# Recording order of a two-layer convolution kernel: norms, loads and the pieces of the convolution

## The chip, the cores and the metric

The kernel runs on one core of a Trainium2 chip. The metric is the device time in microseconds (us) of one execution. The engines are TensorE (PE, with its weight loads PEld), VectorE (DVE), ScalarE (ACT), GpSimd (POOL) and SyncE (SP), which issues all the large transfers here.

## What is computed

Everything is float32. The input x has the shape (4, 256, 256, 64): batch, height, width, channels. The first layer is a Fourier branch and a depthwise convolution, each with a residual:

```python
h = _pw(_ln(x, g1, b1), w_te, b_te)                       # 64 -> 128 channels
F = jnp.fft.fft2(h.astype(jnp.complex64), axes=(1, 2))
fr = jnp.concatenate([jnp.real(F), jnp.imag(F)], axis=-1)
fc = jax.nn.gelu(_pw(fr, w_fc, b_fc), approximate=False)  # 256 -> 256
re, im = (fc[..., :HID], fc[..., HID:])
sp = jnp.real(jnp.fft.ifft2(re + 1j * im, axes=(1, 2)))
x1 = x + _pw(sp, w_tp, b_tp)                              # 128 -> 64
h2 = _pw(_ln(x1, g2, b2), w_fe, b_fe)                     # 64 -> 128
d = lax.conv_general_dilated(h2, w_dw, ...) + b_dw        # 3x3 depthwise
d = jax.nn.gelu(d, approximate=False)
return x1 + _pw(d, w_fp, b_fp)                            # 128 -> 64
```

The second layer treats the height as time. It takes a moving average over 25 steps as the trend, filters the rest in the frequency domain with one complex 128x128 matrix a channel, and adds the trend. For each channel this is one real 256x256 matrix, which the kernel builds from w_real and w_imag and then applies.

## The kernel before

The work falls into five streams, written as Python generators, which record instructions piece by piece and yield between pieces.

`forward_h(b)` (L312) goes over a batch in 32 chunks of 8 columns of the width. `load(q)` (L320) issues two transfers for xt and records the layer norm's statistics: the square on ACT (L295), two reductions and two small operations on DVE (L296 to L299). `transform(q)` (L331) records the scale on GpSimd, a power for rstd (L305) and a product that scales xt in place (L306), then four additions on DVE (xb L338 and xt L340), the matmuls ps_y (L345), two copies to yt on ACT (L352) and the stores to y_d (L357). xt has three buffers, xb one. One piece holds `load(q)` and then `transform(q - 1)`.

`spectral(b)` (L367) goes over 65 pairs of rows of the spectrum, in groups of two pairs. A group is loaded from y_d (L380), and GpSimd writes a negated copy (L399). A pair passes through `transform_w` (ps_x, L414, and a copy to xs), `mix` (ps_p, L434; the copy L447, sums L449, gelu L450, and half of L452 on DVE and half on GpSimd) and `project` (ps_z, L482), each one pair behind the other. `back_w` (ps_u, L499) closes a group with sums on DVE (L510, L511) and stores to u_d (L513). An iteration has three pieces; `transform_w` and `back_w` share the first.

`convolution(b)` (L548) goes over 32 chunks of 8 columns. `back_h(q)` loads uc and x1 (L561, L562), runs the matmuls ps_s (L569), adds them to x1 on DVE (L577, L581) and records the statistics. `to_channels(q)` scales into xn on GpSimd, sets the edges of tt to zero with a GpSimd memset (L591), transposes on TensorE (ps_t, L596), copies to tt on ACT (L603) and forms four row sums td on DVE (L610 to L615). `conv_first` and `conv_rest` make the convolution from four `product`s (ps_h, L629 and L639) whose results DVE folds into h (L660, L661, L667); `activate` is the gelu (L681), `finish` projects with ps_f (L690), adds x1 into st on DVE (L702) and stores to x2_d every second chunk. An iteration has five pieces, and a chunk is in flight for five iterations.

`matrices` (L742) makes the second layer's matrix for each of 64 channels: `first(c)` is ps_v and a copy to vs on ACT, `second(c)` is ps_m, an addition to mt on DVE (L780) and a store. `second` follows one channel behind `first`. The last part, behind the `seq` pool (L828), applies the matrices and isn't part of the change.

All tiles in PSUM come from one pool of eight banks (L118).

What sets the order is `spaced` and `merge` (L795, L800): each stream's pieces get equally spaced due times, in units of one batch, and the piece with the smallest due time is recorded next. Convolution b runs from b to b + 1, beside spectral b + 1 and forward transform b + 2. The recorded order is the order of priority; each engine then has its own queue[...].

Of the kernel before, what the change touches and what calls it, by code (L numbers as in the profile page):

```python
# [10 lines left out]
F32 = mybir.dt.float32  # L11
# [6 lines left out]
P = 128  # L18
N = 256
C = 64  # L20
# [86 lines left out]
def conv_seq_kernel(ctx: ExitStack, tc: tile.TileContext, a: dict, tables: bass.AP, out: bass.AP):  # L107
    nc = tc.nc
# [203 lines left out]
    def forward_h(b, pool):  # L312

        WH = 4
        y_d = spill.tile([P, N, 2, C], F32, tag="y_d", name=f"y_d_{b}")
        y_ds[b] = y_d
        flat = lambda t: t.rearrange("p t f w c -> p (t f w) c")
        chunks = {}

        def load(q):  # L320

            xt = pool.tile([P, 2, 2, WH, C], F32, tag="xt", name=f"xt_{b}_{q}", bufs=3)
            for hf in range(2):
                w0 = hf * P + q * WH
                nc.sync.dma_start(
                    xt[:, :, hf],
                    x[b, :, w0 : w0 + WH, :].rearrange("(t p) w c -> p t w c", p=P),
                )
            chunks[q] = xt, statistics(pool, flat(xt), f"{b}_{q}")

        def transform(q):  # L331
            n = f"{b}_{q}"
            xt, var = chunks.pop(q)
            xb = pool.tile([P, 2, 2, WH, C], F32, tag="xb", name=f"xb_{n}", bufs=1)
            yt = pool.tile([P, 2, WH, 2, C], F32, tag="yt", name=f"yt_{n}")
            scale(pool, flat(xt), flat(xt), var, n)
            for i, op in enumerate((ALU.add, ALU.subtract)):
                nc.vector.tensor_tensor(xb[:, :, i], xt[:, :, 0], xt[:, :, 1], op)  # L338
            for i, op in enumerate((ALU.add, ALU.subtract)):
                nc.vector.tensor_tensor(xt[:, i], xb[:, 0], xb[:, 1], op)  # L340
            for m in range(2):
                ps = bank(f"ps_y_{n}_{m}")

                for i in range(2):
                    nc.tensor.matmul(  # L345
                        ps[i * C : (i + 1) * C],
                        dh[:, m, i * C : (i + 1) * C],
                        xt[:, i].rearrange("p f w c -> p (f w c)"),
                        start=True,
                        stop=True,  # L350
                    )
                nc.scalar.copy(  # L352
                    yt[:, :, :, m, :], ps.rearrange("p (f w c) -> p f w c", f=2, c=C)
                )
            for par in range(2):
                w0 = par * P + q * WH
                nc.sync.dma_start(y_d[:, w0 : w0 + WH], yt[:, par])  # L357

        NCH = P // WH
        for q in range(NCH + 1):  # L360
            if q < NCH:
                load(q)
            if q >= 1:
                transform(q - 1)
            yield

    def spectral(b, pool):  # L367
# [163 lines left out]
        for i in range(len(prs) + 3):  # L531
            if i < len(prs):
# [4 lines left out]
                transform_w(pr)  # L537
            if 0 <= i - 3 < len(prs) and prs[i - 3]["last"]:
                back_w(prs[i - 3]["g"])
# [8 lines left out]
    def convolution(b, pool):  # L548
# [5 lines left out]
        x1s, ts, stores = {}, {}, {}  # L554
        rows = lambda t: t.rearrange("p t w c -> p (t w) c")

        def back_h(q):
# [6 lines left out]
            )  # L564

            pss = [bank(f"ps_s_{n}_{i}") for i in range(2)]
# [15 lines left out]
            x1s[q] = x1, statistics(pool, rows(x1), n)  # L582

        def to_channels(q):

            n = f"c_{b}_{q}"
            x1, var = x1s[q]
            xn = pool.tile([P, 2, W, C], F32, tag="xn", name=f"xn_{n}", bufs=1)
            scale(pool, rows(x1), rows(xn), var, n)
            tt = pool.tile([P, NP, N + 2], F32, tag="tt", name=f"tt_{b}_{q}", bufs=1)  # L590
            nc.gpsimd.memset(tt[:, :, 0 : N + 2 : N + 1], 0.0)  # L591
            for j in range(0, NP, 2):
# [12 lines left out]
                )  # L605

# [76 lines left out]
        def finish(q, i0):  # L683
# [16 lines left out]
            x1 = x1s[q][0]  # L700
# [13 lines left out]

        for q in range(NCH + 4):
            if q < NCH:
                back_h(q)
            yield
            if 0 <= q - 1 < NCH:
                to_channels(q - 1)  # L720
            yield
            done = 0 <= q - 4 < NCH
            now = 0 <= q - 3 < NCH
# [3 lines left out]
            if done:  # L727
                finish(q - 4, 0)
            if now:
                conv_rest(q - 3, 0)  # L730
            yield
# [3 lines left out]
            if done:  # L735
                finish(q - 4, 2)
                del gs[q - 4], x1s[q - 4]
            yield
# [3 lines left out]
    def matrices(pool):  # L742
# [17 lines left out]
        def first(c):  # L760
# [3 lines left out]
            vs = pool.tile([P, 2, N], F32, tag="vs", name=f"vs_{c}", bufs=3)  # L764
# [18 lines left out]
        pending = None  # L783
        for c in range(C):
            if c % CG == 0:
                load(c)
            done = first(c)
            if pending is not None:
                second(*pending)
            pending = done  # L790
            yield
        second(*pending)
        yield
# [21 lines left out]
    with tc.tile_pool(name="fwd", bufs=2) as fwd, tc.tile_pool(name="mix", bufs=2) as mixing:  # L815
        at = {
            all_batches(spectral, mixing, 3 * 68, -1.0, -0.08): -1.0,
            all_batches(forward_h, fwd, 33, -2.05, -1.1): -2.05,
        }
        with tc.tile_pool(name="matrices", bufs=2) as pool:  # L820
            at[spaced(matrices(pool), C + 1, -2.05, -1.1)] = -2.05
            merge(at, -1.0)
        with tc.tile_pool(name="conv", bufs=2) as conv:
            at[all_batches(convolution, conv, 5 * 36, 0.0, 1.0)] = 0.0
# [86 lines left out]
```

## Time and profile before

| | |
|---|---|
| median of 3 runs | 5897.06 us (5895.28 to 5897.61) |
| the profiled execution | 5904.44 us, span 5902.7 us |
| granted TensorE clock, mean | 0.945 of full speed |
| busy: PE, PEld, DVE, ACT, POOL | 92%, 59%, 65%, 39%, 30% of the span |
| moved by DMA | 653.73 MB, 111 GB/s over the span |

Busy times are of the engines' instructions. A matmul's end is modelled and its neighbours overlap, so a PE that is busy is not one at its peak; the granted clock is a column of its own in the views cut by time. Waits are shown as an engine's idle time ahead of an instruction, with the instruction on another engine that ended it.

### The profile page before, as it was taken

Reading aid. Unit: us, or ns where it says so; the run is one execution under the profiler, and the core shown is the slowest. Engines: PE = TensorE matmul, PEld = TensorE weight load, DVE = VectorE, ACT = ScalarE, POOL = GpSimd, SP = SyncE. Lnnn points to the kernel's source line nnn. Section 1 sums busy time; section 2 is a strip of 40 time slices with the busy share of each in tenths; the row PEclk is TensorE's granted clock in tenths of the full one; section 3 lists DMA queues with packets and bytes.
Section 4 is the critical chain, followed back from the end, with each engine's and each line's share of the span. In section 5 each row is a group of like instructions: output and inputs, shape, how many; then the busy total and the mean of one; then the engine's idle time right before and its main releaser. Section 6 shows DMA issues by size and latency. Waiting matters only on the chain.

```text
span 5902.7 us, 72524 instructions
## 1 busy us (share of the span) xinstructions
PE 5436.0 (92%) x27467; PEld 3470.5 (59%) x27467; DVE 3814.1 (65%) x6039; ACT 2276.8 (39%) x3162; POOL 1744.8 (30%) x1038
## 2 busy tenths in 40 slices
PE   7878988798999989899999989999999989997999
PEld 3446656556665656566656556676667656664444
DVE  5555656576777767676777766677766667774221
ACT  2224545444443434344444434444444422221211
POOL 3443333343333233333333322222222223330000
PEclk9988989899999989999999889999999999998999
DMA  4552323322322322322322222222222122224998
GB/s 151 164 166 86 101 86 100 97 83 90 104 97 86 99 73 91 113 79 93 100 97 88 91 79 83 72 82 76 90 76 86 59 78 86 86 86 132 334 321 270
DMA packets 654916, 653.73 MB, mean 111 GB/s; under 512 B 31117, under 2 KB 506719, under 8 KB 654440
## 3 DMA queue, kind: packets, MB, share of 16 engines
q1 hardware_dynamic: 654568, 649.09, 34.7%
q8 instruction: 219, 3.59, 0.3%
q14 instruction: 129, 1.06, 0.1%
HBM read 363.76 MB, written 285.21 MB: 110 GB/s over the span
## 4 chain that ended last, share of the span: by engine, by line
PE 54%; issue 16%; POOL 12%; DVE 10%; DMA 3%; ACT 3%; SPq 1%; POOLq 0%; DVEq 0%; ACTq 0%
PE ps_h L629 12%; PE ps_o L851 7%; PE ps_h L639 7%; PE ps_f L690 6%; PE ps_z L482 5%; PE ps_x L414 4%; POOL rstd L305 4%; PE ps_u L499 4%; POOL xt L306 3%; PE ps_p L434 3%; PE ps_s_c L569 3%; DVE g L449 2%; POOL rstd_c L305 2%; DVE xb L338 2%; PE ps_y L345 1%
## 5 line engine op out<-in xcount | busy, mean ns | idle before, releaser
L629 PE MATMUL ps_h<-td,wc_main 128*128 128x512 f32 x2048 | 1063.1, 642 | 77.6 <-DVE h L661 72.4
L450 ACT ACTIVATE g<-g,b_fc 128x1024 f32<-128x1024 f32 (+1 forms) x520 | 591.9, 1142 | 767.9 <-DVE g L449 767.6
L305 POOL TENSOR_TENSOR rstd_c<-var_c,minus_half 128x16 f32<-128x16 f32 x128 | 419.6, 3278 | 1316.2 <-DVE var_c L299 1224.6
L452 POOL TENSOR_TENSOR g<-g 128x512 f32<-128x512 f32 x260 | 334.0, 1284 | 1448.2 <-ACT g L450 1389.5
L449 DVE TENSOR_TENSOR g<-ps_p,g 128x512 f32<-128x512 f32 x1040 | 687.5, 681 | 75.6 <-ACT g L447 65.4
L639 PEld LDWEIGHTS ps_h<-td,wc_half 64*128 64x128 f32 x4032 | 426.8, 193 | 487.6 <-issue 421.1
L482 PEld LDWEIGHTS ps_z<-w_tp,g 128*128 128x128 f32 x4064 | 509.0, 203 | 225.5 <-POOL g L452 70.3
L482 PE MATMUL ps_z<-w_tp,g 128*128 128x64 f32 x4064 | 548.1, 290 | 99.8 <-POOL g L452 64.8
L629 PEld LDWEIGHTS ps_h<-td,wc_main 128*128 128x128 f32 x2048 | 367.7, 199 | 420.7 <-issue 314.8
L639 PE MATMUL ps_h<-td,wc_half 64*128 64x128 f32 (+1 forms) x4032 | 604.7, 416 | 0.0
L338 DVE TENSOR_TENSOR xb<-xt 128x512 f32<-128x512 f32 x256 | 214.8, 866 | 566.4 <-POOL xt L306 549.0
L667 DVE TENSOR_TENSOR h<-h,ps_h 128x512 f32<-128x512 f32 x512 | 338.6, 683 | 346.7 <-PE ps_h L639 346.6
L690 PE MATMUL ps_f<-w_fp,h 128*128 128x64 f32 x4096 | 525.2, 283 | 38.4 <-DVE h L661 35.8
L434 PE MATMUL ps_p<-xs,wp 64*128 64x512 f32 (+1 forms) x2080 | 531.0, 610 | 28.4 <-DVE h L661 22.7
L681 ACT ACTIVATE h<-h,b_conv 128x1024 f32<-128x1024 f32 x256 | 281.5, 1142 | 690.9 <-DVE h L679 690.4
L690 PEld LDWEIGHTS ps_f<-w_fp,h 128*128 128x128 f32 x4096 | 493.5, 197 | 91.1 <-issue 47.3
L414 PE MATMUL ps_x<-tab,yb 128*128 128x128 f32 x4064 | 537.9, 288 | 0.8 <-DVE ut L511 0.8
L414 PEld LDWEIGHTS ps_x<-tab,yb 128*128 128x128 f32 x4064 | 498.6, 200 | 53.6 <-issue 25.9
L851 PE MATMUL ps_o<-xc,mt 128*128 128x512 f32 x1024 | 450.1, 602 | 42.7 <-issue 21.8
L499 PE MATMUL ps_u<-zt,tab 128*128 128x256 f32 x2048 | 474.5, 386 | 12.0 <-ACT zt L485 11.9
L305 POOL TENSOR_TENSOR rstd<-var,minus_half 128x16 f32<-128x16 f32 x128 | 379.3, 2963 | 322.3 <-DVE var L299 320.2
L447 ACT COPY g<-ps_p 128x512 f32<-128x512 f32 (+1 forms) x520 | 297.8, 582 | 451.2 <-PE ps_p L434 448.9
(120 smaller groups left out, 6863.8 us busy)
## 6 DMA issues: line engine op xcount, KB each, us to landing
xt<-in_x_dram SPq DMA_DIRECT2D x256, 256.0 KB, 3.7
y_d<-yt SPq DMA_DIRECT2D x256, 256.0 KB, 3.3
yb<-y_d SPq DMA_DIRECT2D x256, 256.0 KB, 3.3
x_c<-in_x_dram SPq DMA_DIRECT2D x128, 512.0 KB, 4.8
u_d<-ut SPq DMA_DIRECT2D x256, 256.0 KB, 2.3
uc_c<-u_d SPq DMA_DIRECT2D x128, 512.0 KB, 4.5
x_d<-st SPq DMA_DIRECT2D x128, 512.0 KB, 3.9
xc<-x_d SPq DMA_DIRECT2D x64, 1024.0 KB, 10.3
```

The costliest lines, as they stand in the source:

```text
L305: nc.gpsimd.tensor_tensor(rstd, var, minus_half.to_broadcast([P, n]), ALU.pow)
L414: nc.tensor.matmul(ps[:, j * N + t * P : j * N + (t + 1) * P], blk[:, t, k, lo : lo + 2 * C], tb[:, t, :], start=i == 0, stop=i == 1,)
L434: nc.tensor.matmul(ps[:, :nf], wp[rows, cols], rhs[rows], start=True, stop=r == 1 or not pr["special"],)
L449: nc.vector.tensor_tensor(g[:, i], pss[0][:, :nf], g[:, 1], op)
L450: nc.scalar.activation(g, g, AF.Gelu, bias=b_fc[:, half : half + 1])
L482: nc.tensor.matmul(zv[:, j, 2 * t + r, :], lhs(d, j, t), w_tp, start=True, stop=True)
L499: nc.tensor.matmul(ps[:, r * KG * C : (r + 1) * KG * C], tb[:, t, :], zt[:, t, ri].rearrange("p k c -> p (k c)"), start=ri == 0, stop=ri == 1,
L629: nc.tensor.matmul(pss[par], wc_main[:, par, k, :], ts[q][:, k].rearrange("p j i -> p (j i)"), start=True, stop=False,)
L639: nc.tensor.matmul(pss[par][:, s * P : (s + n) * P], wc_half[lo : lo + C, k, :], td[lo : lo + C, k, at : at + n, :].rearrange("p j i -> p ...
L667: nc.vector.tensor_tensor(g, g, m, (ALU.add, ALU.subtract)[r])
L690: nc.tensor.matmul(pv[:, t, 2 * i + par, :], gs[q][par][:, i0 + i, t * P : (t + 1) * P], w_fp, start=True, stop=True,)
L851: nc.tensor.matmul(ps[:, :nf], mt[:, c % CM, t, to * P : (to + 1) * P], xc[:, t, b0 : b0 + nb2, :, c % CG, :], start=t == 0, stop=t == 1,)
```

## The change

The forward transform's norm, statistics and scale together, becomes a step of its own, `norm(q)`. One chunk takes two pieces: first `transform(q - 1)`, then `load(q + 1)` and `norm(q)`. The first load comes ahead of the loop.

The spectral part yields between `transform_w` and `back_w`, so an iteration has four pieces.

In the convolution `load` is separated from `back_h` and recorded a chunk ahead; the norm is separated from `back_h` and `to_channels` and stands two pieces after `back_h`; the row sums are separated from the transposes. An iteration has nine pieces. The tile tt is allocated once a batch, and its edges are zeroed once by DVE instead of once a chunk by GpSimd.

In `matrices`, `second` follows two channels behind `first`, and vs has four buffers. The counts of pieces given to `spaced` follow.

```diff
@@ forward_h
-            chunks[q] = xt, statistics(pool, flat(xt), f"{b}_{q}")
+            chunks[q] = xt
+
+        def norm(q):
+            n = f"{b}_{q}"
+            xt = flat(chunks[q])
+            scale(pool, xt, xt, statistics(pool, xt, n), n)
 
         def transform(q):
             n = f"{b}_{q}"
-            xt, var = chunks.pop(q)
+            xt = chunks.pop(q)
...
-            scale(pool, flat(xt), flat(xt), var, n)
...
+        load(0)
         for q in range(NCH + 1):
-            if q < NCH:
-                load(q)
             if q >= 1:
                 transform(q - 1)
+            yield
+            if q + 1 < NCH:
+                load(q + 1)
+            if q < NCH:
+                norm(q)
             yield
@@ spectral
                 transform_w(pr)
+            yield
             if 0 <= i - 3 < len(prs) and prs[i - 3]["last"]:
                 back_w(prs[i - 3]["g"])
@@ convolution
-        def back_h(q):
+        def load(q):
...
+            x1s[q] = x1
+            ucs[q] = uc
+
+        def back_h(q):
+
+            n = f"c_{b}_{q}"
+            uc, x1 = ucs.pop(q), x1s[q]
...
-            x1s[q] = x1, statistics(pool, rows(x1), n)
+
+        def norm(q):
+            n = f"c_{b}_{q}"
+            xns[q] = pool.tile([P, 2, W, C], F32, tag="xn", name=f"xn_{n}", bufs=1)
+            scale(pool, rows(x1s[q]), rows(xns[q]), statistics(pool, rows(x1s[q]), n), n)
+
+        tt = pool.tile([P, NP, N + 2], F32, tag="tt", name=f"tt_{b}", bufs=1)
+        nc.vector.memset(tt[:, :, 0 : N + 2 : N + 1], 0.0)
 
         def to_channels(q):
 
-            n = f"c_{b}_{q}"
-            x1, var = x1s[q]
-            xn = pool.tile([P, 2, W, C], F32, tag="xn", name=f"xn_{n}", bufs=1)
-            scale(pool, rows(x1), rows(xn), var, n)
-            tt = pool.tile([P, NP, N + 2], F32, tag="tt", name=f"tt_{b}_{q}", bufs=1)
-            nc.gpsimd.memset(tt[:, :, 0 : N + 2 : N + 1], 0.0)
+            xn = xns.pop(q)
...
+
+        def row_sums(q):
...
+        load(0)
         for q in range(NCH + 4):
-            if q < NCH:
-                back_h(q)
-            yield
-            if 0 <= q - 1 < NCH:
-                to_channels(q - 1)
-            yield
-            done = 0 <= q - 4 < NCH
-            now = 0 <= q - 3 < NCH
+            new, old = q < NCH, 0 <= q - 4 < NCH
+            before, now = 0 <= q - 1 < NCH, 0 <= q - 3 < NCH
             if now:
                 conv_first(q - 3)
             yield
-            if done:
+            if old:
                 finish(q - 4, 0)
+            yield
+            if before:
+                to_channels(q - 1)
+            yield
             if now:
                 conv_rest(q - 3, 0)
+            yield
+            if before:
+                row_sums(q - 1)
+            yield
+            if new:
+                back_h(q)
             yield
             if now:
                 conv_rest(q - 3, 1)
                 activate(q - 3)
-            if done:
+            yield
+            if new:
+                norm(q)
+            yield
+            if old:
                 finish(q - 4, 2)
                 del gs[q - 4], x1s[q - 4]
+            if q + 1 < NCH:
+                load(q + 1)
             yield
@@ matrices
-            vs = pool.tile([P, 2, N], F32, tag="vs", name=f"vs_{c}", bufs=3)
+            vs = pool.tile([P, 2, N], F32, tag="vs", name=f"vs_{c}", bufs=4)
...
-        pending = None
-        for c in range(C):
-            if c % CG == 0:
-                load(c)
-            done = first(c)
-            if pending is not None:
-                second(*pending)
-            pending = done
-            yield
-        second(*pending)
-        yield
+        pending = []
+        for c in range(C + 2):
+            if c < C:
+                if c % CG == 0:
+                    load(c)
+                pending.append(first(c))
+            if c >= 2:
+                second(*pending.pop(0))
+            yield
@@ the counts of pieces
-            all_batches(spectral, mixing, 3 * 68, -1.0, -0.08): -1.0,
-            all_batches(forward_h, fwd, 33, -2.05, -1.1): -2.05,
+            all_batches(spectral, mixing, 4 * 68, -1.0, -0.08): -1.0,
+            all_batches(forward_h, fwd, 2 * 33, -2.05, -1.1): -2.05,
...
-            at[spaced(matrices(pool), C + 1, -2.05, -1.1)] = -2.05
+            at[spaced(matrices(pool), C + 2, -2.05, -1.1)] = -2.05
...
-            at[all_batches(convolution, conv, 5 * 36, 0.0, 1.0)] = 0.0
+            at[all_batches(convolution, conv, 9 * 36, 0.0, 1.0)] = 0.0
```

More of the change, by code (lines that the diff above doesn't have):

```diff
@@ L553, in convolution @@
         NP = W // 2
-        x1s, ts, stores = {}, {}, {}
+        x1s, ucs, xns, ts, stores = {}, {}, {}, {}, {}
         rows = lambda t: t.rearrange("p t w c -> p (t w) c")
-        def back_h(q):
+        def load(q):
             n = f"c_{b}_{q}"
@@ L699, in finish @@
                 stores[s] = pool.tile([P, 2, C, SW], F32, tag="st", name=f"st_{b}_{s}")
-            x1 = x1s[q][0]
+            x1 = x1s[q]
             for t in range(2):
```

## The prediction

> **What bounds the kernel now.** I read the page's busy table first (PE 92%, DVE 65%, no other engine above 40%), then the windows view cut at the stage borders of the trace, then the waits, then the timeline of one stage that repeats. The borders are the copies at L391, which open a batch of the spectral part (417, 1118, 2365, 3641 us), and the last edge columns at L677 (4780, 5405 us).
>
> ```profile
> core 0: us, PE busy (x) PEld busy (x) DVE busy (x) ACT busy (x) POOL busy (x), PEclk, DMA share, GB/s
> 0.00:417.00 417.00, 322.54 (x1051) 173.08 (x1051) 227.75 (x393) 102.51 (x167) 169.98 (x78) 0.93 0.50 158
> 417.00:1118.00 701.00, 603.62 (x3298) 433.35 (x3300) 428.80 (x637) 353.93 (x509) 252.43 (x159) 0.90 0.32 98
> 1118.00:2365.00 1247.00, 1140.39 (x6108) 745.90 (x6105) 887.34 (x1385) 525.52 (x726) 432.85 (x257) 0.93 0.29 90
> 2365.00:3641.00 1276.00, 1185.45 (x6396) 775.57 (x6394) 912.65 (x1436) 535.88 (x740) 425.40 (x254) 0.94 0.29 92
> 3641.00:4780.00 1139.00, 1131.66 (x6499) 781.05 (x6499) 784.15 (x1254) 494.75 (x668) 280.54 (x196) 0.99 0.25 79
> 4780.00:5405.00 625.00, 601.68 (x3097) 364.34 (x3096) 476.20 (x810) 176.31 (x226) 183.56 (x95) 0.98 0.22 76
> ```
>
> Call these stages A to F (the last stage, up to 5903, is G). To see how far each is from a full TensorE I take the pace of its matmul groups from the timeline, start of a group to start of the next with nothing waiting: ps_y 1.87 us a forward chunk; ps_x 1.89, ps_p 1.82, ps_z 1.85 and half of ps_u's 3.55, so 7.4 a spectral pair; ps_s 1.82, ps_t 0.92, four products of 2.98 and ps_f 3.7, so 18.4 a convolution chunk; 3.45 a channel of the matrices. Per batch that is 60 (32 chunks), 480 (65 pairs) and 586 (32 chunks); the matrices are 221. Work against time taken: A 281 and 28 of preparation against 417, excess 108; B 540 against 701, 161; C 1126 against 1247, 121; D 1126 against 1276, 150; E 1066 against 1139, 73; F 586 against 625, 39. TensorE is the bound, and some 650 us are lost to it before G. Part of that is its clock: the clock is 0.99 in E, where it hardly stops, and 0.90 in B.
>
> The difference between D and E is one stream: E has no forward transform. Where it runs, DVE is blocked by one wait (in us, times, longest), which has no entry in E or F; TensorE's own waits of the whole run stand under it.
>
> ```profile
> DVE xb L338 <- POOL xt L306: 549.0, 123, 7.7
> ```
>
> ```profile
> PE ps_h L629 <- DVE h L661: 72.4, 18, 5.3
> PE ps_z L482 <- POOL g L452: 64.8, 34, 5.2
> PE ps_m L772 <- ACT vs L765: 47.8, 23, 3.9
> PE ps_f L690 <- DVE h L661: 35.8, 9, 5.7
> PE ps_y L345 <- issue: 25.9, 3, 10.2
> PE ps_p L434 <- DVE h L661: 22.7, 15, 4.4
> ```
>
> The reader is to see that TensorE's own waits name DVE's h (L661), which frees its PSUM banks, while DVE's queue stands 4.5 us at a time (549/123) behind an xb that wants GpSimd's scaled xt. How that comes about shows in A, DVE first and GpSimd after it:
>
> ```profile
> 189.77 1.29 DVE L338 TENSOR_TENSOR xb<-xt 128x512 f32<-128x512 f32 x2 [4.99 <-POOL xt L306]
> 191.10 1.29 DVE L340 TENSOR_TENSOR xt<-xb 128x512 f32<-128x512 f32 x2
> 192.31 0.68 DVE L780 TENSOR_TENSOR mt<-t,ps_m 128x512 f32<-128x512 f32 x1
> 192.91 1.21 DVE L296 TENSOR_REDUCE total<-xt 128x16 f32<-128x1024 f32 x1
> 194.04 1.21 DVE L298 TENSOR_REDUCE squares<-sq 128x16 f32<-128x1024 f32 x1
> ```
>
> ```profile
> 196.21 2.89 POOL L305 TENSOR_TENSOR rstd<-var,minus_half 128x16 f32<-128x16 f32 x1 [6.47 <-DVE var L299]
> 199.18 1.90 POOL L306 TENSOR_TENSOR xt<-xt,rstd 128x1024 f32<-128x1024 f32 x1
> ```
>
> The two engines take turns: 6.4 us of DVE, then 5.0 us (2.89 + 1.90 and handing over) of GpSimd, 11.35 us a chunk, while TensorE has 8.8 us of work in it (two channels and a ps_y).
>
> [...]xb is 866 ns on average against a median of 691, so the overlap that the change wants has a price of up to some 0.2 us an instruction.
>
> **The change part by part.**
>
> Forward transform. The scale (rstd and xt) leaves the piece that uses it and is recorded half a chunk earlier, with the statistics; the load stands a chunk before them, at SP behind the y_d stores of the chunk before, which wait for yt. No instruction is added. What can go is the 549 us of DVE's wait. The order of each engine in the trace is not simply the recorded one (at 2517.66 us squares L298 runs ahead of total L296, recorded the other way), so the record is a priority and part of the wait will stay. Per stage, with the xb waits 167, 137, 126 and 124 us in A to D:
> - C and D: I let them come to E's excess over work, 1139/1066 = 1.068, so 1203 each: 44 and 73 us saved. E is the same program without the stream that blocks.
> - B: the DVE load is heavier for its length, and ps_z waits for g L452 besides (62 us), which shares GpSimd with the scale. I take half of its excess: 80.
> - A: DVE's and GpSimd's turns can overlap only if the next chunk's reductions stand between a scale and its xb. Three xt buffers allow it. Bounds: 0 (turns stay) and 87 (417 to the 330 that 1.068 gives). I take 25.
>
> Matrices. second(c) comes two channels after first(c), one more vs buffer. It removes up to the 47.8 us of ps_m's wait, all in A. While A is paced by the turns, this saves nothing; it is inside A's 25.
>
> Convolution, pieces. Nine instead of five, no instruction more. Products no longer follow each other without spectral work between, so DVE has longer to free banks; the waits for h L661 (131 us over C and D) are in the 117 already counted. E has none of them, so I count E at 0, with bounds of -15 and +25. norm stands two pieces after back_h and four before to_channels: at some 39 us an iteration about 17 us, against 3 us of reductions and 5.5 us of GpSimd (3.28 + 2.18). If that cover failed, ps_t would wait some of those 5.5 us in each of 128 chunks; now it waits 35 us in all. xn has one buffer, free when the transposes of the chunk before have run, half an iteration earlier.
>
> Convolution, loads. Two DMAs of 512 KB (4.5 us to land) go behind the x2_d stores, which wait for DVE's st, and have most of an iteration. TensorE waits for uc only 7.3 us now: 0 saved.
>
> Edge zeros. 128 GpSimd memsets (13.8 us, with 31.3 us of waiting for td in front) become four on DVE; edge_rows L679 at 0.2 us is the nearest row, so under 1 us. ps_t and ps_z wait 19.5 us for the memset, most of it in F. I take 15.
>
> The yield between transform_w and back_w spreads ps_x and ps_u: 0, inside the above.
>
> Sum: 25 + 80 + 44 + 73 + 15 = 237 us. The profiled execution took 5904.4 us (span 5902.7), so 5667; it lies 7 above the median of the runs, so 5660.
>
> **Rivals.**
>
> All of it: A, B, C and D all come to 1.068 (87 + 124 + 44 + 73) and the memset's 15: 343 us, 5554. For it: DVE is 55 to 72% busy in A to D, so nothing but order stands in the way. Against it: in B and A the loop scale, xb, ps_y, store, next load runs through every engine[...].
>
> The order hardly changes: since the record is only a priority, the scale already runs as soon as var is there (rstd follows var within 0.25 us in A), and xb is still placed right behind it. Then only the memset and some bank waits go, 15 + 25: 5857.
>
> Slower: the scale, now early, stands in GpSimd's queue in front of the subtraction g L452 for which ps_z waits. There are 256 norms, each 4.8 to 5.5 us. Today those waits are 65 us in 34 places. If half of the main case's gain (118 us) is still there, it decides from 0.46 us of added waiting a norm (118/256); at 0.85 us, a sixth of a norm, it adds 218 us and the kernel ends 100 us above the 5897. For it: g L452 has 1.27 us of work and sits directly between gelu and ps_z. Against it: ps_z is recorded five spectral pieces after mix, over 20 us in C and D. I put this case at 6000, and at 1.3 us a norm it would be 6110.
>
> **How the numbers follow.** Main case 0.43, all of it 0.12, hardly any 0.22, slower 0.23. Its own range for the main case is 5560 to 5790 (A at its two bounds, B between 40 and 124, E -15 to +25). No change means within 0.2% of 5897, which is what a measurement here can tell. Hardly-any falls faster in 0.13, within in 0.06, slower in 0.03. So faster 0.68, same 0.06, slower 0.26. The range 5520 to 5950 leaves out most of the slower case and the edge of the full one, about 0.2.
>
> **What would show it.** Right: the wait of xb for xt falls from 549 us to below 250, the waits for h L661 from 131 to below 50, PE's clock in C and D rises to about 0.97, the tt memset is gone from GpSimd, D takes about as long as E plus a forward transform. A's period of 11.35 us tells whether the turns ended. Wrong: xb still waits 4 to 5 us a chunk (hardly any), or ps_z waits for g L452 well above 65 us (slower).

## The result and the profile after

The changed kernel takes 5931.2 us (median of 4 runs, 5929.4 to 5932.3) beside 5897.3 us for the kernel before in the same series (4 runs, 5895.3 to 5899.0): ratio 1.0057, 95% interval 1.0040 to 1.0075. It is slower by 34 us (0.6%), where 5660 us, a gain of 237 us, was forecast. The profiled executions have spans of 5930.5 and 5902.7 us, so they show 28 us of it.

The windows view of the changed kernel, cut at the same events as before (the DVE copy of yr, now L399; the last edge columns, now L696):

```profile
core 0: us, PE busy (x) PEld busy (x) DVE busy (x) ACT busy (x) POOL busy (x), PEclk, DMA share, GB/s
0.00:417.00 417.00, 323.24 (x1051) 168.60 (x1051) 227.20 (x394) 102.00 (x166) 166.69 (x75) 0.93 0.49 155
417.00:1122.00 705.00, 604.73 (x3285) 439.86 (x3286) 429.48 (x636) 354.91 (x508) 256.23 (x162) 0.89 0.32 99
1122.00:2377.00 1255.00, 1142.36 (x6122) 764.38 (x6122) 857.59 (x1373) 520.85 (x723) 396.58 (x220) 0.92 0.29 90
2377.00:3677.00 1300.00, 1194.39 (x6408) 797.17 (x6408) 892.41 (x1445) 537.14 (x742) 411.58 (x226) 0.93 0.29 90
3677.00:4808.00 1131.00, 1118.37 (x6493) 775.29 (x6493) 782.08 (x1259) 490.87 (x670) 263.23 (x165) 0.99 0.25 79
4808.00:5426.00 618.00, 592.35 (x3058) 358.15 (x3057) 464.44 (x803) 174.32 (x225) 153.58 (x64) 0.97 0.24 77
```

A is unchanged at 417 us, B 4 us longer, C 9 and D 24 longer, E 8 to 9 shorter. (The border between F and G in the prediction, 5405 us, lay 6 us behind the last edge columns, which start at 5398.8; with the right border F took 618 us before and takes 618 now.) The loss therefore sits in C and D, where the forward transform runs beside the convolution; with B these were the stages that were to gain most. TensorE's clock there did not rise to 0.97; it fell from 0.93 and 0.94 to 0.92 and 0.93.

Next the waits of the changed kernel, first the one entry that was to shrink, then the head of TensorE's own list (us in total, times, longest):

```profile
DVE xb L342 <- POOL xt L306: 740.2, 128, 9.5
```

```profile
PE ps_z L490 <- POOL g L460: 66.9, 34, 4.7
PE ps_t L613 <- POOL xn_c L306: 65.7, 10, 10.4
PE ps_t L613 <- DVE h L680: 53.2, 16, 7.3
PE ps_y L349 <- issue: 40.0, 5, 12.4
PE ps_m L802 <- DVE mt L810: 34.3, 22, 2.2
PE ps_p L442 <- DVE ut L519: 31.7, 14, 3.3
PE ps_h L648 <- DVE ut L519: 24.9, 4, 7.5
```

The reader is to see two things. The wait of DVE for the scaled xt grew from 549 to 740 us, in all 128 chunks. And the products of the convolution no longer wait for their own banks: ps_h, ps_f and ps_p for h (131 us before) are gone from this list, as forecast. But other matmuls wait for other DVE work instead (ps_t for h, ps_p and ps_h for ut): together the three come to 110 us, and ps_z for h, a little further down the list, adds 19.5. So 131 us of waiting have become 129 under other names: DVE, which frees these banks, still stands at xb.

How the wait grew is in the timeline of D. GpSimd first (start, length, engine, line, what; idle time before it in brackets), then DVE, then the one matmul group of that stretch that waited:

```profile
2536.09 2.90 POOL L305 TENSOR_TENSOR rstd_c<-var_c,minus_half 128x16 f32<-128x16 f32 x1 [18.47 <-DVE var_c L299]
2539.06 2.35 POOL L306 TENSOR_TENSOR xn_c<-x_c,rstd_c 128x1024 f32<-128x1024 f32 x1
2541.38 2.89 POOL L305 TENSOR_TENSOR rstd<-var,minus_half 128x16 f32<-128x16 f32 x1
2544.35 1.91 POOL L306 TENSOR_TENSOR xt<-xt,rstd 128x1024 f32<-128x1024 f32 x1
```

```profile
2538.25 0.16 DVE L299 SCALAR_TENSOR_TENSOR var<-var,squares 128x16 f32<-128x16 f32 x1
2538.36 0.69 DVE L457 TENSOR_TENSOR g<-ps_p,g 128x512 f32<-128x512 f32 x1
2538.97 0.68 DVE L460 TENSOR_TENSOR g<-g 128x512 f32<-128x512 f32 x1
2546.29 2.75 DVE L342 TENSOR_TENSOR xb<-xt 128x512 f32<-128x512 f32 x2 [6.63 <-POOL xt L306]
```

```profile
2551.83 3.65 PE L490 MATMUL ps_z<-w_tp,g 128*128 128x64 f32 x16 [6.22 <-DVE h L680]
```

DVE makes var at 2538.25, does two more instructions and comes to xb. GpSimd has only begun the convolution's norm: the forward norm stands behind it and starts 3 us after var, so the two norms run back to back for 10 us and DVE stands for 6.63 us. Behind xb in DVE's queue wait the h additions that free PSUM banks: their matmuls on ps_h have ended by 2542.9, and they start at 2550.28, after the 6.63 us and the four additions of transform. TensorE then stands 6.22 us for one of them.

Stage A has the same turns as before:

```profile
191.68 1.29 DVE L342 TENSOR_TENSOR xb<-xt 128x512 f32<-128x512 f32 x2 [4.99 <-POOL xt L306]
...
203.04 1.29 DVE L342 TENSOR_TENSOR xb<-xt 128x512 f32<-128x512 f32 x2 [4.99 <-POOL xt L306]
```

The period is 203.04 - 191.68 = 11.36 us, against 11.35 before: the sign that the prediction named for the turns not having ended.

Where xb really stands in DVE's queue can be counted in the traces, as the DVE instructions that ran between the last var of a chunk and its xb (means over the 32 chunks of a batch, batches 0 to 3):

```
before                 0.4   1.1   2.1   2.6
after                  0.3   1.3   1.1   1.4
forward part alone     0.2   1.1   2.0   2.5
convolution alone      0.4   1.1   1.5   2.1
```

The scale and the statistics are now recorded a piece of work ahead of xb, yet xb runs as close behind var as before. In the kernel before, the statistics of the next chunk were even recorded ahead of xb, and xb did not run behind them either; the new loop records `transform(q - 1)` first and the next `norm(q)` after it, so it no longer asks for that order. And in batches 2 and 3 the forward rstd stands directly behind an instruction of the convolution's norm on GpSimd in 22 and 23 of 32 chunks, where before it was 8 and 8.

### The profile page after: what moved, and what is told of

The parts are those of the page before. It is cut to its first block, busy times and chain, and to the rows that moved or that the text cites. A ratio compares the mean times of both kernels' runs of the same rounds, so it can differ in the third digit from the quotient of the medians.

```text
span 5930.5 us, 72294 instructions
## 1 busy us (share of the span) xinstructions
PE 5433.2 (92%) x27467; PEld 3507.2 (59%) x27467; DVE 3752.8 (63%) x6043; ACT 2270.3 (38%) x3162; POOL 1647.9 (28%) x910
## 5 line engine op out<-in xcount | busy, mean ns | idle before, releaser
L648 PE MATMUL ps_h<-td,wc_main 128*128 128x512 f32 x2048 | 1014.1, 618 | 33.0 <-DVE ut L519 24.9
L458 ACT ACTIVATE g<-g,b_fc 128x1024 f32<-128x1024 f32 (+1 forms) x520 | 591.5, 1143 | 669.0 <-DVE g L457 668.5
L342 DVE TENSOR_TENSOR xb<-xt 128x512 f32<-128x512 f32 x256 | 199.4, 812 | 740.2 <-POOL xt L306 740.2
L490 PE MATMUL ps_z<-w_tp,g 128*128 128x64 f32 x4064 | 565.5, 296 | 107.8 <-POOL g L460 66.9
L490 PEld LDWEIGHTS ps_z<-w_tp,g 128*128 128x128 f32 x4064 | 528.1, 209 | 221.6 <-POOL g L460 72.1
L305 POOL TENSOR_TENSOR rstd_c<-var_c,minus_half 128x16 f32<-128x16 f32 x128 | 370.8, 2897 | 885.1 <-DVE var_c L299 799.2
L658 PE MATMUL ps_h<-td,wc_half 64*128 64x128 f32 (+1 forms) x4032 | 588.3, 407 | 0.0
L422 PE MATMUL ps_x<-tab,yb 128*128 128x128 f32 x4064 | 557.0, 294 | 9.3 <-DVE g L457 8.7
L422 PEld LDWEIGHTS ps_x<-tab,yb 128*128 128x128 f32 x4064 | 518.8, 207 | 48.0 <-DVE g L457 10.6
L709 PEld LDWEIGHTS ps_f<-w_fp,h 128*128 128x128 f32 x4096 | 506.9, 201 | 66.4 <-issue 19.5
L507 PEld LDWEIGHTS ps_u<-zt,tab 128*128 128x128 f32 x2048 | 384.5, 193 | 74.7 <-ACT zt L493 11.7
```

Of the source, the lines that this page charges most:

```text
L305: nc.gpsimd.tensor_tensor(rstd, var, minus_half.to_broadcast([P, n]), ALU.pow)
L422: nc.tensor.matmul(ps[:, j * N + t * P : j * N + (t + 1) * P], blk[:, t, k, lo : lo + 2 * C], tb[:, t, :], start=i == 0, stop=i == 1,)
L458: nc.scalar.activation(g, g, AF.Gelu, bias=b_fc[:, half : half + 1])
L490: nc.tensor.matmul(zv[:, j, 2 * t + r, :], lhs(d, j, t), w_tp, start=True, stop=True)
L507: nc.tensor.matmul(ps[:, r * KG * C : (r + 1) * KG * C], tb[:, t, :], zt[:, t, ri].rearrange("p k c -> p (k c)"), start=ri == 0, stop=ri == 1,
L648: nc.tensor.matmul(pss[par], wc_main[:, par, k, :], ts[q][:, k].rearrange("p j i -> p (j i)"), start=True, stop=False,)
```

## The experiments

18 kernels were run. Ratios are to the kernel before, run beside each. In the table A to D are stage lengths and the last column is the whole wait of xb, all in us.

| kernel | time | ratio, 95% interval | A | B | C | D | xb waits |
|---|---|---|---|---|---|---|---|
| before | 5897 | 1 | 417 | 701 | 1246 | 1276 | 549 |
| after | 5931 | 1.0057 [1.0040, 1.0075] | 417 | 705 | 1255 | 1300 | 740 |
| fwd_only | 5921 | 1.0039 [1.0026, 1.0052] | 421 | 698 | 1252 | 1285 | 512 |
| conv_only | 5839 | 0.9901 [0.9888, 0.9915] | 418 | 702 | 1210 | 1260 | 676 |
| fwd_conv | 5853 | 0.9927 [0.9915, 0.9939] | 422 | 699 | 1219 | 1267 | 706 |
| yield_only | 5913 | 1.0032 [1.0020, 1.0043] | 418 | 711 | 1241 | 1279 | 585 |
| no_fwd | 5901 | 1.0009 [1.0000, 1.0017] | 417 | 709 | 1240 | 1283 | 702 |
| no_yield | 5858 | 0.9939 [0.9925, 0.9953] | 418 | 707 | 1215 | 1264 | 699 |
| no_mat | 5933 | 1.0065 [1.0049, 1.0080] | 422 | 711 | 1255 | 1297 | 744 |
| order_before | 5771 | 0.9787 [0.9774, 0.9800] | 338 | 630 | 1255 | 1287 | 14 |
| order_fwd | 5573 | 0.9452 [0.9437, 0.9467] | 365 | 646 | 1150 | 1184 | 5 |
| order_conv | 5619 | 0.9527 [0.9514, 0.9539] | 353 | 638 | 1172 | 1208 | 6 |
| order_after | 5505 | 0.9335 [0.9323, 0.9348] | 366 | 645 | 1119 | 1138 | 25 |
| order_no_yield | 5500 | 0.9334 [0.9320, 0.9348] | 361 | 640 | 1125 | 1140 | 14 |
| mult_before | 5527 | 0.9383 [0.9361, 0.9404] | 336 | 615 | 1134 | 1181 | 166 |
| mult_after | 5461 | 0.9267 [0.9252, 0.9283] | 344 | 624 | 1109 | 1151 | 253 |
| mult_no_yield | 5474 | 0.9290 [0.9272, 0.9307] | 342 | 623 | 1119 | 1157 | 234 |
| newton_before | 5633 | 0.9539 [0.9516, 0.9562] | 378 | 620 | 1166 | 1207 | 262 |
| newton_after | 5582 | 0.9454 [0.9437, 0.9472] | 375 | 625 | 1145 | 1186 | 239 |
| newton_order_after | 5469 | 0.9265 [0.9251, 0.9280] | 358 | 606 | 1120 | 1150 | 8 |

### One part alone, and the order forced

The first theory was that the part with the norms back to back, the convolution's, does the harm, and that xb's place in DVE's queue is what would have to change. Two kernels have one part of the diff each:

```
fwd_only  = before + the hunks of forward_h (load a chunk ahead, norm(q) a piece
            before transform(q), one more yield, 2 * 33 pieces)
conv_only = before + the hunks of the convolution (load, norm and row_sums apart,
            nine pieces, one tt per batch)
```

> The kernel before with the forward transform's part of the change alone (norm as a step of its own, load a chunk ahead). Queue theory (an engine's queue follows the builder's own idea of readiness, so the recorded step moves nothing): xb stands 1 to 3 DVE instructions behind its var as before, xb's wait for xt stays at 530 to 570 us, the time is 5890 to 5905 us. Forward theory (the new step itself does the harm): 5920 us or more. Prediction's reasoning (the step takes DVE's wait away): below 5800 us.

> The kernel before with the convolution's part alone (nine pieces, load and norm as steps, edge zeros once a batch). Queue theory: the convolution's norm now stands right in front of the forward norm in GpSimd's queue in about 20 of 32 chunks of the stages C and D, xb's wait for xt rises to 650 us or more, the time is 5920 to 5945 us. Piece theory (banks and xn are not ready where the pieces put the transposes): the same time, but xb's wait stays near 550 us and ps_t waits over 100 us. Forward theory: 5885 to 5900 us.

The first theory fell. The convolution part alone gains 58 us (0.0099 x 5897) though xb's wait rises from 549 to 676; the forward part alone, the one that was to remove the wait, loses 23 us and leaves xb waiting 512 us for the scale and 72 us more that the waits list of that kernel books to the memset of tt (549 and 17 us before). The two norms back to back therefore make xb wait longer, but the longer wait is not by itself the loss: conv_only has them in 20 of 32 chunks as well, and gains.

The other two put the four additions of transform on DVE behind the statistics of the next chunk. No instruction is added and none waits for new data. In the traces of before and order_before TensorE runs the same instructions in the same order; DVE's order is another, and ACT's and GpSimd's differ in a few places (152 of 3162 and 42 of 1038):

```
+            last[q] = nc.cur_bb.bb.instructions[-1]
...
+            with tc.issue_after(last.pop(q + 1)) if q + 1 in last else nullcontext():
                 for i, op in enumerate((ALU.add, ALU.subtract)):
                     nc.vector.tensor_tensor(xb[:, :, i], xt[:, :, 0], xt[:, :, 1], op)
                 for i, op in enumerate((ALU.add, ALU.subtract)):
                     nc.vector.tensor_tensor(xt[:, i], xb[:, 0], xb[:, 1], op)
```

In order_before that is all; order_after is the changed kernel with it, and its forward loop in the order load(q + 1), norm(q), yield, transform(q - 1), yield.

> The kernel before, with one thing forced: DVE's four additions of chunk q (xb, xt) are queued behind the last operation of chunk q+1's statistics. Same instructions, no new data wait. Queue theory: the additions stand 8 to 38 DVE instructions behind their var, xb's wait for xt falls from 549 to below 100 us, stage A's period of 11.35 us falls to about 9, the time is 5680 to 5790 us. If the wait of xb costs nothing because TensorE is bound elsewhere: 5880 to 5900 us.

> The changed kernel with the same order forced (the forward pieces are norm q, then transform q-1). Queue theory: xb's wait falls from 740 to below 120 us, and the time to within 0.7% of the kernel before with that order, 5670 to 5800 us; the two norms side by side on GpSimd no longer matter. Piece theory: the loss stays, at 30 us or more above the kernel before with that order, and ps_t still waits over 100 us.

Between var and xb there are now 9.6, 18.9, 42.5 and 43.8 DVE instructions in order_before, counted as above. The waits of that kernel:

```profile
PE ps_y L347 <- issue: 135.0, 13, 11.9
PE ps_y L347 <- DVE xt L342: 81.5, 11, 11.2
PE ps_y L347 <- ACT g L452: 58.2, 6, 9.7
DVE xb L340 <- POOL xt L306: 13.8, 5, 4.1
```

xb's wait is gone (13.8 us), and A and B give back 79 and 71 us, of the 108 and 161 us of excess that the prediction counted there. C and D give back nothing; they are 8 and 11 us longer. TensorE now stands at ps_y: 135.0 + 81.5 + 58.2 = 275 us, up to 11.9 us at once. The profile shows no releaser for the 135.0; the reading that ps_y, in one piece with transform, reaches TensorE before its xt is there is borne out by the runs that move it. In order_after, with the pieces of the forward transform half a chunk apart and nine pieces in the convolution, C and D come down too, and the time is below both expectations. Its windows:

```profile
1010.00:2130.00 1120.00, 1093.95 (x6190) 733.28 (x6191) 901.45 (x1397) 529.05 (x731) 431.70 (x227) 0.98 0.32 102
2130.00:3268.00 1138.00, 1120.76 (x6374) 746.97 (x6373) 921.33 (x1439) 535.35 (x738) 418.86 (x222) 0.99 0.32 102
```

They are near the 1126 us of work that the prediction counted (C is below it, so the count was a little high), and the clock is 0.98 and 0.99. DVE does the same work in less time, so it was never short of capacity. This kernel differs from the changed one in two things, the forced order and the order of the two forward pieces, and no run has the new order of the pieces without the force. order_before differs from before in the forced order alone.

### Which part of the change, with and without the forced order

The next theory was that the forward part does its harm beside the new convolution, and that with the order forced each part would show its worth.

```
no_fwd     = after, with the hunks of forward_h undone
fwd_conv   = before + the hunks of forward_h + those of the convolution
order_fwd  = order_before + the forward loop of order_after
order_conv = order_before + the hunks of the convolution
```

> The changed kernel with the forward transform's part undone (convolution, spectral yield and matrices as changed). The forward part alone cost 0.4% and the convolution's part alone gained 1.0%, yet together with the rest they lose 0.6%. If the forward part does the harm, more so beside the new convolution: 5820 to 5850 us, like the convolution's part alone. If the spectral yield or the matrices do it: 5900 us or more.

> The kernel before with the forward and the convolution's part, without the spectral yield and the matrices. If the forward part does the harm beside the new convolution: 5910 to 5935 us, xb's wait over 400 us in C and D. If the two just add up: 5855 to 5870 us, and the spectral yield or the matrices cost the remaining 60 us.

> The kernel before with the forced order of DVE and the forward part (norm q in a piece of its own, transform q-1 half a chunk later). With the forced order alone, C and D gained nothing (1255 and 1287 us), since ps_y waited up to 11.9 us at TensorE. Theory: recording the transform half a chunk behind the next norm gives TensorE's queue the room, ps_y's waits in C and D fall from 264 to below 60 us, C and D come to 1120 to 1170 us each, the time is 5520 to 5600 us. Rival (it is the nine pieces that give the room): C and D stay above 1220 us, the time is above 5720 us.

> The kernel before with the forced order and the nine pieces of the convolution, the forward pieces as before. Theory: ps_y still waits over 150 us in C and D, the time is 5700 to 5770 us. Rival: C and D at 1120 to 1170 us, 5520 to 5600 us.

That theory fell as well: no_fwd stays at 5901 us, 62 above conv_only although it has no forward part either, and forward and convolution together stand at 5853 us, 44 below before. The harm was in something else, which no_fwd has and conv_only and fwd_conv lack. With the order forced, both parts are worth much: 5771 to 5573 with the forward part (its pieces in the order of order_after), to 5619 with the convolution's, to 5505 with everything. order_fwd came out at the time expected: TensorE stands 67 us at ps_y in place of 275. order_conv came between its two expectations, with 92 us at ps_y: the nine pieces alone remove most of it, too.

### The remaining two parts

```
no_yield       = after, without the yield between transform_w and back_w
no_mat         = after, with matrices as before (second one channel late, vs bufs 3)
yield_only     = before + that one yield
order_no_yield = order_after without that yield
```

> The changed kernel without the yield between transform_w and back_w (spectral part as before, three pieces an iteration). Forward and convolution parts together took 5853 us, the whole change 5931. If the yield costs the 78 us: 5840 to 5865 us, with C and D at about 1219 and 1267 us. If the matrices do: 5915 to 5940 us.

> The changed kernel with the matrices as before (second one channel behind first, three vs buffers). If the yield costs the 78 us: 5920 to 5940 us. If the matrices do: 5840 to 5865 us.

> The kernel before with the yield alone. If the yield does harm by itself: 5940 to 5980 us. If only beside the new convolution: 5885 to 5910 us.

> The changed kernel with the forced order and without the yield. If the yield's harm passes through the blocked DVE queue, it is gone once xb no longer waits: 5490 to 5520 us, as with the yield. If it is independent of that: 5420 to 5450 us.

The matrices do nothing (1.0065 against 1.0057, intervals overlapping): ps_m waited 47.8 us for ACT's vs before, now it waits 34.3 us for DVE's mt. The yield is what turns the gain into a loss. The ratios make a ledger: convolution -58 us, forward part on top +15, matrices +7 (from fwd_conv to no_yield, intervals overlapping), yield +70, sum +34. The yield costs 19 us alone (0.0032 x 5897) and 70 beside the rest, but nothing where the order is forced (0.9335 against 0.9334). So its price is not work: it is not paid where xb hardly waits.

On TensorE the price shows only in small part as waits. C and D of no_yield:

```profile
1125.00:2339.00 1214.00, 1110.69 (x6127) 742.07 (x6126) 864.60 (x1380) 521.92 (x724) 398.65 (x221) 0.94 0.29 93
2339.00:3603.00 1264.00, 1165.10 (x6407) 774.89 (x6405) 893.43 (x1440) 535.77 (x741) 412.87 (x225) 0.94 0.29 92
```

The two stages are 77 us shorter than in the changed kernel, but TensorE's idle time in them (length less PE busy) is 202 us against 218, only 16 less. The granted clock is 0.94 in both, against 0.92 and 0.93. An estimate of what the clock takes is the length times what it lacks to 1: 149 us here, 191 in the changed kernel, so some 42 of the 77 us (the clock's two digits leave that open by 12 us either way in each kernel).

### The norm made cheap, queues untouched

What was open was whether the length of GpSimd's norm is really what xb, and through it the yield, pays for, or the place of ps_u on TensorE, which the yield moves from directly behind ps_x to near ps_t. Three kernels have a multiplication where the power stood, and leave out the reciprocal root by that; in the traces every engine runs the same instructions in the same order as in the parent kernel (but for 4 of the 27467 matmuls in mult_before):

```
-        nc.gpsimd.tensor_tensor(rstd, var, minus_half.to_broadcast([P, n]), ALU.pow)
+        nc.gpsimd.tensor_tensor(rstd, var, minus_half.to_broadcast([P, n]), ALU.mult)
```

> The changed kernel with a multiplication in place of the power in every norm's rstd (the output scale is then not the reciprocal root, so this part of the computation is left out); every queue holds the same instructions in the same order. Theory (DVE stands behind xb until GpSimd has made the norm's power, 2.9 us, and product, 1.9 us, and in C and D often the convolution's norm before it): the power shrinks to some 0.3 us, the wait of xb falls from 740 us to about 300, stages C and D from 1256 and 1300 to about 1190 each, the whole to about 5700. Rival (the length of GpSimd's norm is beside the point; the place of ps_u in TensorE's queue and the bank waits cost the time): under 40 us gained, 5890 or more.

> The same multiplication in place of the power in the changed kernel without the yield between transform_w and back_w, queues as in that kernel. Theory: the yield's price is paid through the blocked DVE queue, so with shorter norms it shrinks from 73 us to 35 or less: about 5670 beside 5700. Rival (the yield's price comes from where ps_u stands on TensorE, whatever DVE does): the difference to the run with the yield stays 60 to 85 us.

> The same multiplication in place of the power in the kernel before, queues as there. Theory: the wait of xb falls from 549 us to about 220 and the time by about 0.6 of what forcing the order gave (126 us), more in A and B, where the turns of DVE and GpSimd are 11.35 us and become about 8.8: about 5800. Rival: under 40 us, 5860 or more.

The rstd line of mult_after in the tile view (duration in ns, min/median/max):

```profile
L305 POOL TENSOR_TENSOR rstd<-var,minus_half x128: 205/216/712, 38.0 to 3198.3; 128x16 f32<-128x16 f32 x128
```

and the same line of the changed kernel:

```profile
L305 POOL TENSOR_TENSOR rstd<-var,minus_half x128: 2890/2900/3383, 37.3 to 3643.8; 128x16 f32<-128x16 f32 x128
```

2.7 us less for each norm, and the kernel before falls by 370 us and the changed one by 470. Both were expected to gain less, 100 and 230 us: what the norm's length costs was underrated. In the kernel before the gain is 81, 86, 112 and 95 us in A to D, where the forward norm runs, and 12 us in E and F together, which have the convolution's norm alone. So it comes with the forward norm, though not all of it need pass through xb: ps_z's wait for g on GpSimd falls too, from 64.8 to 36.8 us. Stage E is also a control for the values. It takes 1136 us in mult_before and 1139 before (1123 and 1131 in the changed pair), so other values in the tiles change little there; for A to D this is not shown by itself. The order of the two kernels turns round: the change now gains 66 us (5527 to 5461) where it lost 34. And the yield costs nothing: 5461 us with it, 5474 without, where it had been 70 us. Each kernel has the queues of its parent, so the place of ps_u alone does not cost the 70 us; it does so only beside norms that hold GpSimd 2.7 us longer. The multiplication shortens the forward and the convolution's norm alike, and no run shortens one of them alone. How the moved ps_u makes DVE's standing longer, from 699 us in no_yield to 740, and lowers the clock, stays open.

### The root made elsewhere

In these three the norm is computed in full. VectorE makes the root from a seed out of the exponent bits and two Newton steps:

```
-        nc.gpsimd.tensor_tensor(rstd, var, minus_half.to_broadcast([P, n]), ALU.pow)
+        nc.vector.tensor_scalar(
+            rstd.bitcast(bits), var.bitcast(bits), -0.5, float(0x5F3759DF), ALU.mult, ALU.add
+        )
+        for _ in range(2):
+            nc.vector.tensor_tensor(step, rstd, rstd, ALU.mult)
+            nc.vector.scalar_tensor_tensor(step, step, -0.5, var, ALU.mult, ALU.mult)
+            nc.vector.scalar_tensor_tensor(rstd, step, 1.5, rstd, ALU.add, ALU.mult)
```

> The kernel before with the reciprocal root made on VectorE: a seed from the exponent bits and two Newton steps, seven small instructions of about 0.2 us (the edge rows, L679, take 0.19) in place of GpSimd's power of 2.9 us; the result is the same. Theory (the length of var to xt in front of xb is what counts): the way is 1.4 + 1.9 us in place of 2.9 + 1.9, but the 1.4 us stand on DVE, so less than the cheap multiplication gave (5527): about 5650. Rival (DVE, with 256 times 1.4 us more, becomes the bound itself): 5850 or more.

> The changed kernel with the same root on VectorE. Theory: xb no longer waits for a convolution's power on GpSimd, so the change gains here as it did with the multiplication (66 us less than the kernel before with the same root): about 5590. Rival (what the change gained with the multiplication came from the missing root altogether): no better than newton_before.

> The changed kernel with the forced order, the best so far with 5505 us, and the root on VectorE. There the way from var to xt is covered, so a shorter one gains little, and DVE has 256 times 1.4 us more at 80% busy in C and D: theory about 5500, between 5460 and 5560. Rival (DVE becomes the bound): 5600 or more.

Its price, from the groups of newton_after (busy us and mean ns of one; the line numbers are those of the new statements):

```profile
L313 DVE SCALAR_TENSOR_TENSOR rstd<-step,rstd 128x16 f32<-128x16 f32 x256 | 87.3, 342 | 6.4
L312 DVE SCALAR_TENSOR_TENSOR step<-step,var 128x16 f32<-128x16 f32 x256 | 72.8, 285 | 6.2
L311 DVE TENSOR_TENSOR step<-rstd 128x16 f32<-128x16 f32 x256 | 56.2, 220 | 5.4
...
L306 DVE TENSOR_SCALAR rstd<-var 128x16 int32<-128x16 int32 x128 | 25.5, 200 | 2.3
```

A forward norm costs DVE 0.20 + 2 x (0.22 + 0.285 + 0.342) = 1.9 us, more than the 1.4 expected and a microsecond less than the power, and DVE is busier by some 280 us in the whole run than in mult_after (4068 against 3788). It still pays: 5633 and 5582 us, and the change gains 51 us on it. Here DVE's queue is another (8 to 14 instructions between var and xb in newton_after and 8 to 19 in newton_before, seven of them the root), so these runs say less about the length alone than the three before. With the forced order it is the fastest kernel here that computes the norm in full, 5469 us, 7.35% below the kernel before. The windows of C and D in it:

```profile
964.00:2083.00 1119.00, 1091.50 (x6166) 731.60 (x6166) 964.08 (x1841) 526.02 (x728) 236.12 (x162) 0.98 0.33 102
2083.00:3233.00 1150.00, 1126.38 (x6403) 751.75 (x6403) 984.03 (x1877) 535.45 (x740) 235.54 (x162) 0.99 0.33 102
```

They are no shorter than in order_after (D is 12 us longer); the 36 us come from A and B, which give 8 and 39 us (358 and 606 us against 366 and 645). In C and D, where the forced order puts over 40 DVE instructions between var and xb, a shorter way gains nothing; in B, with 19 between them, it still does.

No run makes the root on ScalarE. The changed kernel has two table loads there, at L795 and at L458, 1283 ns each; what a root between the gelus would add is not shown.

## Why the prediction was wrong

**The view of the bound was right.** TensorE is the bound and what it loses in A to D comes for the most part from DVE standing at xb. order_after takes that wait away and ends at 5505 us, mult_after shortens it and ends at 5461; "all of it" was put at 5554. Against it stands that the wait's length does not set the time by itself: conv_only is faster with 676 us of it than before with 549.

**The step that failed** is the first term of the forward transform: "What can go is the 549 us of DVE's wait." It was taken from where the scale is recorded. The wait depends on where xb stands on DVE relative to var, and there the change moved nothing: xb stays 0.3 to 1.4 instructions behind on average (0.4 to 2.6 before), and its wait grew to 740 us. The prediction saw the reason (the record is only a priority) and wrote it down as a rival, but still let C and D come to E's ratio of 1.068, on the ground that E lacks the stream that blocks. The change does not take the stream away, so the comparison gave the size of the loss, not of the gain.

**Stage by stage.** A: 25 us forecast, 0 measured, at the lower bound given, with the 11.36 us period. B: 80 forecast, 4 lost. C and D: 44 and 73 forecast, 9 and 24 lost. In A the condition was stated rightly, that the next chunk's reductions must stand between a scale and its xb; three xt buffers allow it, but the new loop records xb ahead of these reductions. order_before does it and gets 79 us there, near the 87 that was the upper bound.

**The yield** was counted as 0, "inside the above". It costs 70 us beside the other parts. This is the second failing term, and it alone decides the sign: without it the changed kernel would be 0.6% faster than before.

**The convolution's pieces** were counted inside C and D and at 0 in E. Alone, with the edge zeros, they gain 36, 16 and 11 us in C, D and E. The mechanism was half right: the waits for h at ps_h, ps_f and ps_p are gone, but ps_t and ps_z now wait 53 and 20 us for h, so h did not fall below the 50 us that the prediction named.

**The norm's cover** of 17 us did not hold everywhere: ps_t now waits 65.7 us for xn_c, in 10 places, where it was 9.5 in two (of the 35 us that ps_t waited in all).

**The edge zeros**, 15 us: the waits for the memset are gone (12.7 us at ps_t in F, 5.8 at ps_z in E), E is 8 to 9 us shorter in all, but F is 618 us as before, since ps_t waits 24.9 us for xn_c there in place of 8.8. No run has this edit by itself.

**The matrices** at nothing was right, and most of the vs wait became a wait for mt.

**The price of overlap** on DVE, up to 0.2 us an instruction, did not come on top: xb takes 812 ns on average in the changed kernel, 866 before. In the traces it is paid by single instructions: an xb with no GpSimd instruction beside it takes 687 ns on average and at most 694 (208 of the 256 in the changed kernel), one with GpSimd busy for over half of its time 1357 ns (the other 48). Before there were 68 of these, at 1365 ns.

**The rivals.** "The order hardly changes" had the mechanism right and the price wrong: it kept 25 us of bank waits and gave the yield nothing. "Slower" had the sign right and the mechanism wrong: ps_z waits 66.9 us for g now and 64.8 before, in 34 places both times. So the norms do not delay g further for TensorE; they delay each other.

## What to carry to other kernels

Ask not how long an instruction waits but what stands behind it in its queue, and before counting a wait as gone, look where the change puts the waiting instruction in the real queue of its engine, since recording the producer earlier helps only if other work comes to stand in between. Then price the chain that the wait consists of: here a product in place of a 128x16 power of 2.9 us, on an engine that is busy for 30% of the span, took some 370 us off a 5897 us kernel, nearly all of it in the stages where DVE stood behind that power. Splitting work into more pieces is worth more once the blocking wait is gone (the convolution's pieces gain 152 us with the forced order and 58 without); before that one more piece, here the yield, can turn the gain into a loss.

## What was not expected of the hardware

On GpSimd a power over 128x16 takes 2900 ns, a multiplication of the same shape 216 ns, and a multiplication over 128x1024 takes 1902 ns: the power costs more than a product of 64 times the size. The granted clock was lower where TensorE stalled, but not in proportion to its idle time. In C and D together TensorE idles 43 us in order_after, at a clock of 0.98 and 0.99, and 218 us in the changed kernel, at 0.92 and 0.93. But in order_before it idles 289 us in two stages that are granted as much as before, where it was 197:

```profile
969.00:2224.00 1255.00, 1103.90 (x6112) 735.28 (x6110) 905.60 (x1387) 531.42 (x726) 451.28 (x259) 0.93 0.28 90
2224.00:3511.00 1287.00, 1149.49 (x6387) 761.26 (x6386) 926.37 (x1436) 541.76 (x739) 439.11 (x254) 0.94 0.28 91
```

The longest single wait of TensorE in C and D does not give the clock either: it is 9.5 us before, 9.6 in the changed kernel, 11.9 in order_before and 7.4 in order_after. What sets the clock stays open.
